# A gated graph network on one core: last two pairs side by side, h kept in place, adj in quarters, its square by seven products

## The chip, the cores and the metric

The kernel runs on one core of one Trainium2 chip. Its engines are TensorE (PE: matmuls; PEld: loading their weights), VectorE (DVE), ScalarE (ACT), GpSimd (POOL) and SyncE (SP, which issues the DMAs here). The metric is device time in microseconds (us), the median of several runs. One more execution was taken with the hardware profiler; all views come from that one.

## The reference, cut to what matters

```python
# x: (32, 512, 128), adj: (512, 512), all fp32
def prop(x): return einsum('ij,bjc->bic', adj, x)
y = [x, A x, A^2 x, A^3 x, A x, A^2 x, A^3 x]          # both adjacency inputs are adj
x = layernorm(x + sum_k y[k] @ W0[k])                   # layer 0
h = x
for _ in range(5):                                      # layer 1
    m  = einsum('nm,bmd->bnd', adj, h)                  # m_in = m_out = m
    u3 = h @ u3_w.T + u3_b
    z  = sigmoid([m, m] @ w3_w.T + w3_b + u3)
    r  = sigmoid([m, m] @ w4_w.T + w4_b + u3)
    hv = tanh([m, m] @ w5_w.T + w5_b + (r * h @ u5_w.T + u5_b))
    h  = (1 - z) * h + z * hv
out = layernorm(x + h)
```

## The kernel before

Two batches make a pair `q` (16 pairs). A tile of one batch is 128 x 512 fp32: nodes on the partitions (four chunks of 128 side by side) or, "turned", channels on the partitions and the 512 nodes along the row.

**Planner.** Nothing is issued directly. Each piece of work is an `Op` with an engine, an assumed length, the operations that it follows, slots that it takes and gives back (`take`, `give`), and a key. `Plan.run` (line 69) goes through time and gives each free engine the ready operation with the lowest key whose slots are free; what it emits in that order is the program's order on every engine. The keys are `32 * q` for a pair, plus 30 and 20 a step inside. Slots are the tiles in `slots` (line 151): eight PSUM banks, `hT` (turned h), `X` (h with nodes on the partitions), `S` (sums for products), `m` (adj times h), `uT`, `rh`, `z`, `rest`, `d` (DRAM), `two` (products under way at a time: 2), `inside` (pairs in layer 1 at a time: 5).

**Products.** `seven` (line 374) multiplies 2 x 2 blocks with seven products instead of eight: each product is two or four matmuls, p1, p3, p5 and p6 add up in one bank, and between them ACT copies its state out (`Q`, c1, c3, c5); DVE adds these copies to the other banks (d2, d5, d7). p3 must wait for c1, p5 for c3, p7 for d5. Its sums (`S`) come from POOL. It is used for adj times x (`adj_product`), for layer 0's weights (line 530) and for adj squared times U (line 586). For the latter adj squared is made once, by 16 matmuls of 128x512 (line 272) from four transposes of adj.

**A step** (`pair`, line 693; `gates`, line 654). u3s times h (line 707), adj times h by `seven`, then for each batch: w4s times m, DVE adds uT (line 664), ACT's sigmoid, DVE times h gives rh; w3s times m, DVE adds uT (line 671), ACT's sigmoid z (line 673) and a second sigmoid of the negated input, `rest` (line 675), that POOL multiplies by h (line 678); w5s times m and u5s times rh into one bank, Tanh (line 685), DVE times z (line 687) and plus rest (line 689) into a new `hT`. For the next step's products h must have its nodes on the partitions: for all pairs but the last by a DVE block transpose and two DMA passes through DRAM (`turn`, line 343), for pair 15 (`TURNED = 15`) by four PE transposes and an ACT copy (lines 739 to 742). After the fifth step POOL adds h0 into a tile `y` (line 752), `norm` (line 309) takes moments on DVE for each of four chunks (lines 318, 319), the power on POOL, and the final scale and shift on ACT (line 328); SP stores.

**Start.** SP loads x of pair 0 (two DMAs), adj in four chunks of 128 rows (line 200), then the weights. DVE makes the sums `T` of adj and the layer 0 weights.

Of the kernel before, what the change touches and what calls it, by code (L numbers as in the profile page):

```python
# [11 lines left out]
ALU = mybir.AluOpType  # L12
PSUM = bass.MemoryType.PSUM

P = 128
# [7 lines left out]
TURNED = 15  # L23
# [17 lines left out]
class Plan:  # L41
# [5 lines left out]
    LATE = {"PE": 0.2, "DVE": 0.1, "ACT": 0.1, "POOL": 0.1, "SP": 0.0, "-": 0.0}  # L47

# [5 lines left out]
    def __call__(self, engine, us, emit, after=(), take=(), give=(), key=0.0, late=None):  # L54
        late = self.LATE[engine] if late is None else late
        op = Op(engine, us, emit, [a for a in after if a is not None], take, give, key, late)
        self.ops.append(op)
        return op
# [62 lines left out]
def gnn_resnorm_kernel(  # L121
# [26 lines left out]
    def tiles(tag, n, shape=(P, N), pool=work):  # L148
# [5 lines left out]
        xg=tiles("xg", 1, (P, 2, NK, P)),  # L154
        xT=tiles("xT", 4),
        tT=tiles("tT", 4),
        U=tiles("U", 2, (P, NK, 2, P)),
        Y=tiles("Y", 2, (P, 2, NK, P)),
        h0=tiles("h0", 5, (P, 2, NK, P)),
        hT=tiles("hT", 10),  # L160
        X=tiles("X", 2, (P, 2, P * NK)),
        m=tiles("m", 7),
        uT=tiles("uT", 4),
        rh=tiles("rh", 3),
        z=tiles("z", 2),
        rest=tiles("rest", 4),
        S=tiles("S", 2, (P, 7, H, P)),
        Q=tiles("Q", 2, (P, 3, HN)),
        v=tiles("v", 5),
        y=tiles("y", 4, (P, NK, P)),  # L170
        two=[None] * 2,
        inside=[None] * 5,
# [18 lines left out]
    def load_x(q):  # L191
        for b in range(2):
            nc.sync.dma_start(plan[f"xg{q}"][:, b], x[2 * q + b].rearrange("(p k) c -> p k c", k=NK))

    def loaded_x(q, key):
        return plan("SP", 0.84, lambda: load_x(q), take=[("xg", f"xg{q}")], key=key, late=3.0)

    x_in = {0: loaded_x(0, -99.0)}
    at_in = [
        plan("SP", 0.46, lambda k=k: nc.sync.dma_start(at[:, k], adjT[:, k]), key=-90.0 + k, late=4.5)  # L200
        for k in (0, 2, 1, 3)
    ]
# [12 lines left out]
    w_of = lambda: plan["w0"].rearrange("p b f -> p (b f)")[:, : 7 * P]  # L215
    w0_in = plan("SP", 0.45, lambda: nc.sync.dma_start(w_of(), w0), take=[("X", "w0")], key=-70.0, late=6.5)

# [10 lines left out]
    w0_ready = plan("DVE", 2.3, layer0_weights, after=[w0_in], give=[("X", "w0")], key=-40.0)  # L228
# [4 lines left out]
    def gate_weight(src, name):  # L233
        halves = lambda: plan[name][:, : 2 * P].rearrange("p (h o) -> p h o", h=2)
        w = const.tile([P, P], F32, tag=name, name=name)
        emit = lambda: nc.sync.dma_start(halves(), src.rearrange("(h c) o -> c h o", c=P))
        got = plan("SP", 0.45, emit, take=[("rh", name)], key=-60.0, late=6.5)
        emit = lambda: nc.vector.tensor_tensor(w, halves()[:, 0, :], halves()[:, 1, :], ALU.add)
        ready.append(plan("DVE", 0.28, emit, after=[got], give=[("rh", name)], key=-30.0))
        return w  # L240
# [18 lines left out]


    an_ready = []
    for km in range(NK):
        emit = lambda km=km: transposes(plan[f"ba{km}"], lambda k: at[:, k, chunk(km)])
        tr = plan("PE", 0.44, emit, after=at_in, take=[("bank", f"ba{km}"), ("m", f"an{km}")], key=20.0)
        emit = lambda km=km: nc.scalar.copy(plan[f"an{km}"], plan[f"ba{km}"])
        an_ready.append(plan("ACT", 0.59, emit, after=[tr], give=[("bank", f"ba{km}")], key=20.0))
    squares, squared = [], []
    for k in range(NK):
        for km in range(NK):

            def emit(k=k, km=km):
                nc.tensor.matmul(  # L272
                    plan[f"bs{k}"],
                    lhsT=plan[f"an{km}"][:, chunk(k)],
                    rhs=at[:, km, :],
                    start=(km == 0),
                    stop=(km == NK - 1),
                )

            squares.append(  # L280
                plan(
                    "PE",
                    0.86,
                    emit,
                    after=an_ready + squares[-1:],
                    take=[("bank", f"bs{k}")] if km == 0 else [],
                    give=[("m", f"an{j}") for j in range(NK)] if k == km == NK - 1 else [],
                    key=21.0,
                )
            )  # L290
        emit = lambda k=k: nc.vector.tensor_copy(at2[:, k, :], plan[f"bs{k}"])
        squared.append(plan("DVE", 0.69, emit, after=squares[-1:], give=[("bank", f"bs{k}")], key=21.0))


    A11, A12 = at2[:, :H, :HN], at2[:, H:, :HN]
    A21, A22 = at2[:, :H, HN:], at2[:, H:, HN:]
    A2_sums = []
    for i, (a, b, op) in enumerate(
        (
            (A21, A22, ALU.add),  # L300
            (at2S[:, 0], A11, ALU.subtract),
            (A11, A21, ALU.subtract),
            (A12, at2S[:, 1], ALU.subtract),
        )
    ):
        emit = lambda i=i, a=a, b=b, op=op: nc.vector.tensor_tensor(at2S[:, i], a, b, op)  # L306
        A2_sums.append(plan("DVE", 0.69, emit, after=squared + A2_sums[-2:], key=21.0))

    def norm(n, name, src_of, dst_of, after, give, key):
# [22 lines left out]
        for i in range(n):  # L332
            got.append(plan("DVE", 0.45, lambda i=i: moments(i), after=after, key=key))
        p = plan("POOL", 1.75, power, after=got, key=key)
        over = []
        for i in range(n):
            last = i == n - 1
            over.append(
                plan("ACT", 0.45, lambda i=i: apply(i), after=[p] + over, give=give if last else [], key=key)
# [3 lines left out]
    def turn(src_of, dst_of, name, after, key, take=()):  # L343
# [15 lines left out]
        t = plan("DVE", 0.7, blocks, after=after, take=[("v", f"v{name}")], key=key)  # L359
# [14 lines left out]
    def seven(name, after, us, terms, product, keep, end, key, take=(), give=()):  # L374
# [4 lines left out]
        Qn = f"Q{name}"  # L379
        banks = {i: f"p{i}{name}" for i in "abc"}  # L380
        half = lambda i: plan[banks[i]][:, :HN]

        def pe(i, bank, first, last, after, take=()):
            left, right, ready = terms[i]
            emit = lambda: product(half(bank), left(), right(), first, last)
            return plan("PE", us, emit, after=list(after) + list(ready), take=take, key=key)

        def out(what, bank, after, *i, give=()):
            engine, us, emit = what(*i)
            return plan(engine, us, lambda: emit(half(bank)), after=after, give=give, key=key)  # L390

        Q_of = lambda i: lambda: plan[Qn][:, i]
        kept = lambda i, bank, after: out(keep, bank, after, i, Q_of(i))
        take = [("two", f"two{name}"), ("Q", Qn), ("bank", banks["a"]), ("bank", banks["c"])] + list(take)
        p1 = pe(0, "a", True, False, after, take=take)
        c1 = kept(0, "a", [p1])
        p2 = pe(1, "b", True, True, [p1], take=[("bank", banks["b"])])
        d2 = out(end, "b", [p2, c1], 0, 0, Q_of(0), give=[("bank", banks["b"])])
        p3 = pe(2, "a", False, False, [c1])
        c3 = kept(1, "a", [p3])  # L400
        p4 = pe(3, "c", True, False, [p1])
        p5 = pe(4, "a", False, False, [c3])
        c5 = kept(2, "a", [p5])
        d5 = out(end, "c", [p4, c5], 1, 1, Q_of(2))
        p6 = pe(5, "a", False, True, [c5])
        c6 = out(end, "a", [p6], 1, 0, None, give=[("bank", banks["a"])])
        p7 = pe(6, "c", False, True, [d5])
        d7 = out(end, "c", [p7, c3, d5, d2], 0, 1, Q_of(1), give=[("bank", banks["c"]), ("Q", Qn), ("two", f"two{name}")])
# [414 lines left out]
```

## Time and profile before

| | |
|---|---|
| median of 3 runs | 1528.29 us (1528.23 to 1528.51) |
| the profiled execution, its own time | 1527.84 us |
| its span, first to last instruction | 1526.0 us |
| busy: PE, DVE, ACT, POOL | 1500.0, 958.8, 830.6, 773.2 us |
| mean granted TensorE clock | 0.996 |
| DMA share | 31.6% of 16 engines |

An engine's busy time is the time in which it works on some instruction; "idle before" is the time just before an instruction, with what ended it. The timeline merges equal neighbours (x4 is four records; an fp32 matmul leaves two, a transpose one). In the table by stretches each row has the stretch, its length, the busy time and number of instructions of each engine, TensorE's granted clock, the DMA share and GB/s. The gates' part of the groups:

```profile
L678 POOL TENSOR_TENSOR rest<-rest,hT 128x512 f32<-128x512 f32 x160 | 202.6, 1270 | 346.0 <-ACT rest L675 330.7
...
L413 ACT COPY Q<-bank 128x256 f32<-128x256 f32 x384 | 143.2, 373 | 293.5 <-PE bank L456 255.8
...
L687 DVE TENSOR_TENSOR bank<-bank,z 128x512 f32<-128x512 f32 x160 | 111.4, 697 | 122.3 <-ACT bank L685 121.2
...
L685 ACT ACTIVATE bank<-bank,hv_b 128x512 f32<-128x512 f32 x160 | 106.0, 663 | 80.4 <-PE bank L659 80.3
...
L673 ACT ACTIVATE z<-bank 128x512 f32<-128x512 f32 x160 | 94.5, 598 | 64.6 <-DVE bank L671 64.4
```

POOL's product of 1270 ns mostly waits for ACT's second sigmoid (330.7 of 346.0 us); all of these run while PE does other pairs' matmuls.

### The profile page before, as it was taken

To read this page: it belongs to the slowest core of one execution; us is meant where nothing else is said; L and a number is where in the kernel's file an instruction comes from. 1 tells how busy PE (TensorE), PEld (TensorE's weight loads), DVE (VectorE), ACT (ScalarE), POOL (GpSimd) and SP (SyncE) were. 2 spreads that over 40 slices of the span, in tenths; PEclk is the share of its full clock that TensorE was granted. 3 is DMA by queue.
4 is the path that set the end of the run, shared out by engine and by line. 5 is a ranking of instruction groups with operands and counts; after the bars stand their busy time and mean duration, and the time that the engine had idled before them with its cause. 6 is when DMAs were issued, how large, how long until landed. Compare 5 with 4: busy or idle time off the path is not lost.

```text
span 1526.0 us, 20599 instructions
## 1 busy us (share of the span) xinstructions
PE 1500.0 (98%) x6200; PEld 1031.2 (68%) x6200; DVE 958.8 (63%) x2039; ACT 830.6 (54%) x1768; POOL 773.2 (51%) x1090
## 2 busy tenths in 40 slices
PE   8999999999999999999999999999999999999995
PEld 6877666666766677676666766677676666766552
DVE  3556576667566665657667566665657666665754
ACT  2364545656465654645656465654546655555644
POOL 3454554545554465554545654464554545634534
PEclk9999999999999999999999999999999999999998
DMA  2122423325144342423414144242423413231220
GB/s 88 50 55 70 111 60 90 106 71 131 44 107 113 76 120 55 125 68 90 132 47 133 43 110 112 72 122 56 130 64 90 132 45 92 59 107 45 61 51 27
DMA packets 160190, 128.19 MB, mean 84 GB/s; under 512 B 18384, under 2 KB 124880, under 8 KB 160080
## 3 DMA queue, kind: packets, MB, share of 16 engines
q1 hardware_dynamic: 160080, 126.89, 31.6%
q8 instruction: 49, 0.80, 0.2%
q14 instruction: 61, 0.50, 0.1%
HBM read 64.42 MB, written 62.39 MB: 83 GB/s over the span
## 4 chain that ended last, share of the span: by engine, by line
PE 96%; issue 1%; DVE 1%; DMA 1%; POOL 1%; ACT 0%; SPq 0%; ACTq 0%; POOLq 0%
PE bank L456 38%; PE bank L659 35%; PE bank L707 9%; PE bank L530 6%; PE bank L586 6%; PE bank L272 1%; PE bank L258 1%; DMA at<-in_adjT 0%; SPq L350 0%; POOL rest L678 0%; DMA v<-d 0%; POOL y L752 0%; DVE st L318 0%; DVE at2S L306 0%; DVE mv L319 0%
## 5 line engine op out<-in xcount | busy, mean ns | idle before, releaser
L678 POOL TENSOR_TENSOR rest<-rest,hT 128x512 f32<-128x512 f32 x160 | 202.6, 1270 | 346.0 <-ACT rest L675 330.7
L456 PE MATMUL bank<-T,S 128*128 128x256 f32 x1392 | 345.1, 380 | 1.5 <-ACT Q L413 1.5
L456 PEld LDWEIGHTS bank<-T,S 128*128 128x128 f32 x1392 | 261.7, 190 | 88.1 <-ACT Q L413 30.3
L413 ACT COPY Q<-bank 128x256 f32<-128x256 f32 x384 | 143.2, 373 | 293.5 <-PE bank L456 255.8
L456 PE MATMUL bank<-at,S 128*128 128x256 f32 x864 | 221.8, 379 | 0.0
L456 PEld LDWEIGHTS bank<-at,S 128*128 128x128 f32 x864 | 160.8, 190 | 45.0 <-issue 25.1
L421 DVE TENSOR_TENSOR m<-bank,Q 128x256 f32<-128x256 f32 x240 | 100.3, 418 | 140.6 <-PE bank L456 94.9
L687 DVE TENSOR_TENSOR bank<-bank,z 128x512 f32<-128x512 f32 x160 | 111.4, 697 | 122.3 <-ACT bank L685 121.2
L664 DVE SCALAR_TENSOR_TENSOR bank<-bank,b4s,uT 128x512 f32<-128x512 f32 x160 | 120.3, 753 | 91.1 <-PE bank L659 86.4
L707 PE MATMUL bank<-hT,u3s 128*128 128x512 f32 x320 | 160.9, 596 | 0.0
L659 PE MATMUL bank<-m,w4s 128*128 128x512 f32 x320 | 157.9, 592 | 0.0
L659 PE MATMUL bank<-m,w5s 128*128 128x512 f32 x320 | 155.0, 592 | 0.0
L659 PE MATMUL bank<-m,w3s 128*128 128x512 f32 x320 | 154.0, 592 | 0.0
L659 PE MATMUL bank<-rh,u5s 128*128 128x512 f32 x320 | 153.2, 592 | 0.0
L685 ACT ACTIVATE bank<-bank,hv_b 128x512 f32<-128x512 f32 x160 | 106.0, 663 | 80.4 <-PE bank L659 80.3
L666 ACT ACTIVATE bank<-bank 128x512 f32<-128x512 f32 x160 | 92.3, 581 | 84.7 <-DVE bank L664 83.9
L712 ACT ACTIVATE uT<-bank,ub3s 128x512 f32<-128x512 f32 x160 | 109.8, 688 | 51.2 <-PE bank L707 48.9
L448 POOL TENSOR_TENSOR S<-X 128x256 f32<-128x256 f32 x128 | 91.7, 727 | 77.7 <-PE bank L456 32.5
L673 ACT ACTIVATE z<-bank 128x512 f32<-128x512 f32 x160 | 94.5, 598 | 64.6 <-DVE bank L671 64.4
L671 DVE SCALAR_TENSOR_TENSOR bank<-bank,b3s,uT 128x512 f32<-128x512 f32 x160 | 118.8, 750 | 11.3 <-PE bank L659 10.8
L667 DVE TENSOR_TENSOR rh<-bank,hT 128x512 f32<-128x512 f32 x160 | 107.7, 681 | 14.5 <-ACT bank L666 13.3
L689 DVE TENSOR_TENSOR hT<-bank,rest 128x512 f32<-128x512 f32 x160 | 107.5, 681 | 7.4 <-POOL rest L678 1.7
(113 smaller groups left out, 2250.6 us busy)
## 6 DMA issues: line engine op xcount, KB each, us to landing
d<-v SPq DMA_DIRECT2D x824, 64.0 KB, 1.8
X<-d SPq DMA_DIRECT2D x150, 256.0 KB, 2.7
v<-d SPq DMA_DIRECT2D x56, 256.0 KB, 2.7
xg<-in_x SPq DMA_DIRECT2D x32, 256.0 KB, 2.7
out<-y SPq DMA_DIRECT2D x32, 256.0 KB, 2.2
at<-in_adjT SPq DMA_DIRECT2D x4, 256.0 KB, 5.3
X<-in_w SPq DMA_DIRECT2D x1, 448.0 KB, 6.4
rh<-in_w SPq DMA_DIRECT2D x3, 128.0 KB, 6.3
```

Source lines behind the costliest of these rows:

```text
L413: return "ACT", 0.37, lambda src: nc.scalar.copy(Q(), src)
L456: nc.tensor.matmul(dst, lhsT=left[:, k, :], rhs=right[:, k, :], start=(first and k == 0), stop=(last and k == H - 1), skip_group_check=True,)
L659: mm = lambda dst, w, src, first, last: nc.tensor.matmul(plan[dst], lhsT=w, rhs=plan[src], start=first, stop=last)
L664: emit = lambda: nc.vector.scalar_tensor_tensor(plan[pr], plan[pr], b4s, plan[uT], ALU.add, ALU.add)
L667: emit = lambda: nc.vector.tensor_tensor(plan[rh], plan[pr], plan[h], ALU.mult)
L671: emit = lambda: nc.vector.scalar_tensor_tensor(plan[pz], plan[pz], b3s, plan[uT], ALU.add, ALU.add)
L678: emit = lambda: nc.gpsimd.tensor_tensor(plan[rest], plan[rest], plan[h], ALU.mult)
L685: emit = lambda: nc.scalar.activation(plan[ph], plan[ph], AF.Tanh, bias=hv_b)
L687: emit = lambda: nc.vector.tensor_tensor(plan[ph], plan[ph], plan[z], ALU.mult)
L689: emit = lambda: nc.vector.tensor_tensor(plan[h_new], plan[ph], plan[rest], ALU.add)
L707: emit = lambda bn=bn, hb=h[b]: nc.tensor.matmul(plan[bn], lhsT=u3s, rhs=plan[hb], start=True, stop=True)
L712: emit = lambda bn=bn, uT=uT: nc.scalar.activation(plan[uT], plan[bn], AF.Identity, bias=ub3s)
```

## The change

It has several parts.

- **Keys.** A pair's key is taken from a list, `KEYS`; a step adds `LONG` = 20. The last two keys are 464 and 478, so pairs 14 and 15 are nearly in step; the others are 22 to 38 apart. `two` goes from 2 to 3, `inside` from 5 to 7. The planner takes an engine to be free a little before an operation is done (`OVERLAP`).
- **Turning h.** `ON_PE = {14: 1, 15: 3}`: PE transposes for pair 14's last step and pair 15's last three; all else by DVE and DMA. After the last step of these two pairs nothing is copied: DVE adds h0 from the PSUM bank.
- **Start.** adj is loaded in quarters (256 rows by 256 columns), in the order x's first half, two quarters, x's second half, two quarters; the first product waits only for its quarter.
- **Square of adj** by `seven`: seven products of four 128x256 matmuls, with four DVE sums of the transposed adj.
- **In place.** `seven` copies its first sum to the result's own tile and adds there (`into`); `Q` is gone. `gates` computes `h + z * (hv - h)` in h's own tile: Tanh, DVE minus h, DVE times z, then plus h on POOL, or on DVE for the last `QUICK` = 2 pairs. `rest`, the second sigmoid and POOL's product are gone, as are the tiles `y`: the result is put in h0's tile. X is held for each batch by itself.

```diff
-TURNED = 15
+ON_PE = {14: 1, 15: 3}
+QUICK = 2
+KEYS = [20.0, 58.0, 80.0, 112.0, 148.0, 180.0, 208.0, 240.0, 272.0, 304.0, 334.0, 366.0, 396.0, 426.0, 464.0, 478.0]
+LONG = 20.0
...
+    OVERLAP = {"DVE": 0.08, "ACT": 0.1, "POOL": 0.04}
...
+        overlap = min(self.OVERLAP.get(engine, 0.0), us / 2)
+        us, late = us - overlap, late + overlap
...
-        xg=tiles("xg", 1, (P, 2, NK, P)),
+        xg=tiles("xg", 2, (P, 2, NK, P)),
...
-        tT=tiles("tT", 4),
+        tT=tiles("tT", 5),
...
-        Y=tiles("Y", 2, (P, 2, NK, P)),
-        h0=tiles("h0", 5, (P, 2, NK, P)),
-        hT=tiles("hT", 10),
-        X=tiles("X", 2, (P, 2, P * NK)),
-        m=tiles("m", 7),
-        uT=tiles("uT", 4),
+        Y=tiles("Y", 4, (P, 2, NK, P)),
+        h0=tiles("h0", 4, (P, 2, NK, P)),
+        hT=tiles("hT", 8),
+        X=tiles("X", 4),
+        uT=tiles("uT", 6),
...
-        z=tiles("z", 2),
-        rest=tiles("rest", 4),
+        z=tiles("z", 4),
+        m=tiles("m", 5),
...
-        two=[None] * 2,
-        inside=[None] * 5,
+        two=[None] * 3,
+        inside=[None] * 7,
...
-        plan("SP", 0.46, lambda k=k: nc.sync.dma_start(at[:, k], adjT[:, k]), key=-90.0 + k, late=4.5)
+    def load_adj(i, j, key):
+        k, c = slice(i * H, (i + 1) * H), slice(j * HN, (j + 1) * HN)
+        emit = lambda: nc.sync.dma_start(at[:, k, c], adjT[:, k, c])
...
+        a = plan("SP", 0.42, emit, take=[("xg", "xg0")], key=-99.0, late=2.9)
+        b = plan("SP", 0.42, lambda: load_x(0, 1), key=-91.0, late=4.0)
...
+    in11, in21 = load_adj(0, 0, -95.0), load_adj(1, 0, -94.0)
+    at_in = [in11, in21, load_adj(0, 1, -90.0), load_adj(1, 1, -90.0)]
...
+    def into(dst, cols, plus=None):
+        def first(i, j):
+            if plus is None:
+                return "ACT", COPY[cols], lambda src: nc.scalar.copy(dst(i, j), src)
+            return "DVE", ADD[cols], lambda src: nc.vector.tensor_tensor(dst(i, j), src, plus(i, j), ALU.add)
+        def second(i, j):
+            return "DVE", ADD[cols], lambda src: nc.vector.tensor_tensor(dst(i, j), src, dst(i, j), ALU.add)
...
+    def square_product(dst, left, right, first, last):
+        for j in range(H):
+            for k in range(H):
                 nc.tensor.matmul(
-                    plan[f"bs{k}"],
-                    lhsT=plan[f"an{km}"][:, chunk(k)],
-                    rhs=at[:, km, :],
...
+                    dst[:, j, :],
+                    lhsT=left[:, k, chunk(j)],
+                    rhs=right[:, k, :],
...
+    _, squared = seven("sq", an_ready, 1.72, terms, square_product, into(dst, N), 21.0, whole, give=give)
...
-        emit = lambda: nc.scalar.activation(plan[rest], plan[pz], AF.Sigmoid, scale=-1.0)
-        t = plan("ACT", 0.59, emit, after=[t, zs], give=[("bank", pz)], key=key + 0.5)
-        emit = lambda: nc.gpsimd.tensor_tensor(plan[rest], plan[rest], plan[h], ALU.mult)
-        keep = plan("POOL", 1.27, emit, after=[t], key=key + 0.5)
...
-        emit = lambda: nc.vector.tensor_tensor(plan[ph], plan[ph], plan[z], ALU.mult)
-        t = plan("DVE", 0.69, emit, after=[t, zs], give=[("z", z)], key=key + 0.8)
-        emit = lambda: nc.vector.tensor_tensor(plan[h_new], plan[ph], plan[rest], ALU.add)
...
+        emit = lambda: nc.vector.tensor_tensor(plan[ph], plan[ph], plan[h], ALU.subtract)
+        t = plan("DVE", 0.69, emit, after=[t], key=key + 0.8)
+        emit = lambda: nc.vector.tensor_tensor(plan[z], plan[ph], plan[z], ALU.mult)
+        t = plan("DVE", 0.69, emit, after=[t, zs], give=[("bank", ph)], key=key + 0.8)
+        engine, us = (nc.vector, 0.69) if quick else (nc.gpsimd, 1.27)
+        emit = lambda: engine.tensor_tensor(plan[h], plan[z], plan[h], ALU.add)
+        return plan("DVE" if quick else "POOL", us, emit, after=[t], give=[("z", z)], key=key + 0.8)
...
+            by_dma = s < STEPS - ON_PE.get(q, 0)
...
+                y = lambda b=b: h0_of(b)
+                if by_dma:
+                    emit = lambda b=b, X_new=X_new, y=y: nc.gpsimd.tensor_tensor(
+                        fit(y(), True), X_new(b), fit(y(), True), ALU.add
+                    )
+                    t = plan("POOL", 1.27, emit, after=[t], give=[("X", Xb)], key=key + 17)
+                else:
+                    emit = lambda y=y, bn=bn: nc.vector.tensor_tensor(
+                        y(), plan[bn].rearrange("p (k c) -> p k c", k=NK), y(), ALU.add
+                    )
+                    t = plan("DVE", 0.69, emit, after=[t], give=[("bank", bn)], key=key + 17)
```

## The prediction, made before the changed kernel was run

> **What bounds the kernel now.** I read three views in this order: the page's sums and chain, the busy time by stretches, then the waits and the timeline at the two ends. First the page:
>
> ```profile
> span 1526.0 us, 20599 instructions
> ...
> PE 1500.0 (98%) x6200; PEld 1031.2 (68%) x6200; DVE 958.8 (63%) x2039; ACT 830.6 (54%) x1768; POOL 773.2 (51%) x1090
> ...
> PE 96%; issue 1%; DVE 1%; DMA 1%; POOL 1%; ACT 0%; SPq 0%; ACTq 0%; POOLq 0%
> ```
>
> TensorE is busy 98% of the span and carries 96% of the chain of waits, so outside the ends a saving must take matmuls away. The stretches (length, then busy time of PE, PEld, DVE, ACT, POOL) show where its 26.0 us of idle time lie:
>
> ```profile
> 0.00:10.00 10.00, 5.29 (x18) 4.31 (x19) 2.10 (x4) 3.21 (x5) 4.19 (x11) 1.00 0.75 238
> 10.00:40.00 30.00, 29.98 (x145) 21.57 (x144) 9.68 (x27) 7.78 (x19) 10.46 (x15) 1.00 0.12 33
> 40.00:60.00 20.00, 18.48 (x129) 16.11 (x128) 12.33 (x33) 4.66 (x12) 9.24 (x14) 1.00 0.27 67
> 60.00:100.00 40.00, 39.95 (x201) 30.30 (x200) 19.93 (x52) 24.66 (x51) 22.61 (x36) 1.00 0.24 61
> 100.00:1400.00 1300.00, 1299.46 (x5367) 895.38 (x5366) 843.34 (x1774) 722.40 (x1547) 674.43 (x947) 1.00 0.34 89
> ...
> 1480.00:1500.00 20.00, 15.75 (x50) 9.22 (x49) 10.45 (x29) 10.83 (x22) 11.14 (x16) 0.91 0.24 69
> 1500.00:1510.00 10.00, 9.08 (x29) 5.08 (x28) 4.88 (x8) 3.46 (x8) 0.19 (x1) 1.00 0.00 0
> 1510.00:1526.00 16.00, 2.97 (x12) 1.22 (x10) 5.68 (x20) 6.70 (x14) 8.20 (x12) 0.71 0.09 33
> ```
>
> From 100 to 1400 us PE is idle 0.54 us: nothing to win there, much to lose. The first 10 us hold 4.7, 40 to 60 hold 1.5, the end holds the rest. What PE waits for after 1440:
>
> ```profile
> PE bank L258 <- DVE hT L689: 6.4, 3, 4.2
> PE bank L456 <- ACT Q L413: 1.8, 4, 0.5
> ```
>
> These are the last pair alone: its transposes wait for its own h, its products for their own copies. The timeline of both ends (start, length, in brackets the wait ahead):
>
> ```profile
> 6.65 2.07 PE L456 MATMUL bank<-at,xg 128*128 128x256 f32 x4 [1.13 <-DMA at<-in_adjT]
> ...
> 1492.73 1.05 PE L258 MATMUL bank<-ident,hT 128*128 128x128 f32 x4 [4.25 <-DVE hT L689]
> ...
> 1501.20 1.13 PE L456 MATMUL bank<-T,S 128*128 128x256 f32 x4 [0.46 <-ACT Q L413]
> ...
> 1502.79 1.13 PE L456 MATMUL bank<-T,X 128*128 128x256 f32 x4 [0.46 <-ACT Q L413]
> ...
> 1510.83 0.66 ACT L685 ACTIVATE bank<-bank,hv_b 128x512 f32<-128x512 f32 x1 [0.33 <-PE bank L659]
> ...
> 1514.48 0.66 PE L258 MATMUL bank<-ident,hT 128*128 128x128 f32 x4 [0.74 <-DVE hT L689]
> ...
> 1521.27 1.65 ACT L328 ACTIVATE y<-y,shift,rstd 128x128 f32<-128x128 f32 x4 [0.26 <-POOL shift L325]
> ```
>
> **What the Trainium skill says.** "TensorE: Matmul & The Clock Gate", section "Wait — 56ns, not 53.3ns?", gives a matmul's spacing as columns by clock plus about 2.5 ns. The trace agrees: 68 records of 256 columns run in 14.68 us on the chain at 991.19, 216 ns each where 213 is the pure array time, two records to a matmul. The section "What's actually happening" has the array at half clock until it has been busy about 3.4 us: at 6.65 four records take 2.07 us, at 1003.11 four take 1.03. That is paid in time, so an earlier start pays it earlier, not less. "PSUM — Partial Sum Buffer", section "Engine vs sequencer instructions", says that ScalarE, VectorE and GpSimd work strictly in order; in the trace DVE's 16 moment instructions of the two batches from 1515.73 to 1519.00 run one behind another. "DMA: Bandwidth & Descriptors", section "Specifications", puts line rate at 512 B and more; adj in quarters has rows of 1 KB instead of 2, so I charge nothing, and no run here shows 1 KB rows.
>
> **The change, part by part**, against the profiled execution's 1527.84 us, of which 1526.0 are the span.
>
> *Square of adj.* A 128x512 matmul takes 0.86 us (from 1504.62 to 1506.34 go two), a 128x256 one 0.43. Out go 16 of the first, 13.8; in come 28 of the second, 12.1: -1.7. The four sums on DVE (0.69 each) and four copies of a whole bank on ACT (about 0.59) lie beside other matmuls: in the new order the products of pair 0 and the w products stand between those of the square.
>
> *Transposes of h on PE.* Before: the last pair's 10 x 4. Now pair 14's last step and pair 15's last three: 8 x 4. Eight fewer at 0.11 (8 go from 13.00 to 13.88): -0.9. What the two new DMA turns cost lies beside the other pair's matmuls. All other matmuls are the same by count.
>
> *Start.* PE's first wait (3.59) is for the first half of x and stays. Then the first product waits 1.13 for a load of adj that stands third in SP's queue; its quarter now stands second, and the transposes of x's second half follow it. The gain is between 0 (if what held the first adj load holds the quarter) and 1.1 (all of it). T's second sum needs the last quarter, at the end of the same 1.5 MB, so that comes no earlier; before it, PE now has 4.3 us of matmul work instead of 3. I take -0.6. The 1.5 us at 40 to 60 are w products with nothing between them; such rows stand in the new order too. I take 0, from -1.5 to +1.5.
>
> *Last two pairs.* In the new order pair 14's matmuls stand between pair 15's nearly to the end; after pair 14's last transposes PE has 12 us left. Before pair 15's earlier turned steps, 4.3 us of matmuls stand between the u5s product and the transposes of the same h. The way back is Tanh 0.66, three DVE operations of 0.69 and some 0.4 of handing over, 3.1: covered by 1.2. The products of the last `seven` have u3s products and pair 14's transposes between them. So all waits after 1440 but the last two go: 8.2 - 1.42 - 0.74 = 6.0 of idle time in seven waits, and each costs more from start to start (1502.79 - 1501.20 is 1.59 for 0.86 of work, 0.73 where 0.46 is idle): 7.4 with 0.2 for each. Late next is DVE: pair 14's two sums and 16 moment instructions, 1.4 + 3.3 us, stand in its queue ahead of pair 15's last gate additions, with two additions of m between; the first u5s would be late by 0.3, the second by 0.7. I take 1.0 back: -6.4, from -8 to -3.
>
> *Behind the last gate.* Before, from the Tanh at 1510.83 to 1526.0: 15.2. Now DVE has six gate operations instead of four, in the order sub, sub, mult, mult, add, add, from 1511.5 at about 0.7: 1515.7. Transposes to 1516.5; the sum from PSUM replaces ACT's copy (0.59) and POOL's sum (1.27), 0.7: 1517.2. Eight pairs of moments at 0.41: 1520.5 (before 1519.0, as DVE was free at 1514.4 and only waited for POOL). POOL 0.4 later for 1.8: 1522.7. ACT then has five of the final operations behind it in its order, not four, at 0.39: 1524.8; and 3.1 for the store, as from 1522.9 to 1526.0: 1527.9. +1.9, from +1.2 to +2.5.
>
> *Gates, all pairs.* ACT loses 160 second sigmoids (94 us of its 831) and POOL's product moves to the end of the chain: for 14 pairs Tanh, sub, mult, then POOL's 1.27 before h can be used, against Tanh, mult, add. Nothing of this is on PE's path unless the order leaves too little between. It leaves, for the inner pairs, 1.4 us at one place and otherwise 3.1 or more beyond that chain before u3s, and 4.5 before the next products (before: 1.9 and 3.7). Where a matmul needs an eviction, only one step of 0.86 stands between at about 400 places, against about 250 before; those 250 cost 0.54 in all. In-place sums change no count: `seven`'s last copy and its DVE additions stay one for one. DVE gets 20 sums for the last two pairs (14 us). I take +0.7 for the middle, from -0.5 to +15.
>
> Sum: -1.7 - 0.9 - 0.6 + 0 - 6.4 + 1.9 + 0.7 = -7.0, so 1520.8 profiled. The profiled execution is 0.45 under the median of the runs, 1528.29; so 1521.3.
>
> **Rivals.** *All gaps close* (0.2): start -1.1, 40 to 60 -1.5, tail -7.4, behind it +1.4, no loss inside: -11.2, 1517. For it: every wait removed has work of the other pair in its place. Against: DVE's queue at the end. *The tail gives it back* (0.15): pair 14's norms and pair 15's gates collide on DVE in both last steps; of 7.4 only 3.4 stay, and the end costs 2.4: -1.7 - 0.9 - 0.6 - 3.4 + 2.4 + 0.7 = -3.5, 1525. For it: before, one such collision made a wait of 4.25 where the bare chain (Tanh, two DVE operations) is 2.4. *DVE and POOL delay the middle* (0.13): h now passes through DVE, DVE and POOL. Of the stretches with 10 us of matmul work, DVE's instructions fill over 0.9 in eight, at most 0.99, before in none (at most 0.89). At 0.2 us for each of the 70 steps of 14 pairs it loses 14 instead of 0.7: +6.3, 1534.6. From 0.15 a step it is slower than before by 0.2%. Against: ACT is freer, POOL's fullest stretch falls from 1.42 to 1.14, and the same kind of order ran 1300 us without a gap.
>
> **How the numbers follow.** Forecast 0.52, with its own range 1517 to 1525. A median of this kernel can tell 0.2%, 3.1 us, from no change: below 1525.2 is faster. The forecast is there nearly always, the second for certain, the third half the time: 0.77. Same: 0.10. Slower: 0.13. The range goes from 1515 to 1531, which leaves under one in ten on each side.
>
> **What would show it.** The stretches after: PE idle under 1.5 between 100 and 1400; no wait of a transpose above 1 us but the last two; PE's wait for adj below 1.1; from the last Tanh to the end about 17. Transposes waiting for h over 2 us before the end speak for the third case, waits for DVE or for POOL's hT spread over the middle for the last. I am wrong if the middle's idle time exceeds 5 us.

## The result and the profile after

| | before | after |
|---|---|---|
| median of 20 runs each | 1528.24 us (1526.98 to 1529.96) | 1525.51 us (1522.49 to 1529.07) |
| ratio after to before, 95% interval | | 0.9984 (0.9977 to 0.9991) |
| the profiled execution, and its span | 1527.84, 1526.0 us | 1526.63, 1524.5 us |

The change wins 2.7 us, where 7 were forecast. First the page of the kernel after: span, busy times, chain of waits.

```profile
span 1524.5 us, 20210 instructions
...
PE 1498.4 (98%) x6216; PEld 1034.4 (68%) x6216; DVE 975.6 (64%) x2068; ACT 753.5 (49%) x1610; POOL 750.6 (49%) x1068
...
PE 90%; DVE 4%; DMA 2%; SPq 2%; ACT 1%; POOL 1%; issue 1%; ACTq 0%; POOLq 0%; DVEq 0%
```

PE is still busy 98% of the span, but its share of the chain fell from 96% to 90%: DVE, DMA and SP's queue now stand on it. Where, the busy time by stretches of the kernel after shows (stretch, length, PE, PEld, DVE, ACT, POOL, clock, DMA share, GB/s):

```profile
0.00:10.00 10.00, 5.25 (x16) 3.93 (x17) 1.30 (x2) 2.83 (x4) 2.95 (x9) 1.00 0.79 244
...
40.00:60.00 20.00, 19.10 (x139) 17.84 (x138) 10.16 (x33) 7.84 (x21) 11.39 (x21) 1.00 0.26 67
...
100.00:1400.00 1300.00, 1295.33 (x5300) 886.79 (x5299) 841.71 (x1775) 652.94 (x1399) 663.39 (x932) 1.00 0.33 88
...
1480.00:1500.00 20.00, 20.00 (x79) 13.36 (x78) 15.66 (x33) 9.76 (x19) 3.23 (x5) 1.00 0.00 0
```

Between 1480 and 1500 PE has no gap left, where it had 4.25 us. Between 100 and 1400 it is idle 4.67 us, where it was 0.54. Idle time is less than what is lost, so the table below counts from the start of each PE record to the start of the next and takes off the time that its columns need at full clock (213 ns for a record of 256 fp32 columns, as the prediction has it). It is worked out from the records of the two profiles; the wait of 3.6 us ahead of the first record, which both have, is left out, and "last gate" is the start of the last u5s record.

| us | before | after | difference | forecast |
|---|---|---|---|---|
| matmuls and transposes at full clock | 1470.3 | 1467.7 | -2.6 | -1.7 - 0.9 |
| lost, 0 to 100 | 10.3 | 9.8 | -0.5 | -0.6 + 0 |
| lost, 100 to 1400 | 18.2 | 25.1 | +7.0 | +0.7 |
| lost, 1400 to 1450 | 0.4 | 0.7 | +0.3 | |
| lost, 1450 to the last gate | 9.6 | 1.0 | -8.5 | -6.4 |
| behind the last gate's start | 15.0 | 17.8 | +2.9 | +1.9 |

The rows give -1.4, the spans -1.5. (Some 17 us of the middle's loss are the 3 ns by which every record exceeds its columns, in both kernels.) One row is out of line: the middle. PE's waits between 100 and 1400 in the kernel after (line waited for, us, times, longest):

```profile
PE bank L487 <- ACT S L467: 1.4, 2, 1.0
PE bank L487 <- DVE m L352: 1.1, 2, 0.6
PE bank L487 <- DVE tT L352: 0.7, 2, 0.6
PE bank L700 <- DVE rh L708: 0.7, 1, 0.7
PE bank L624 <- DVE v L349: 0.6, 1, 0.6
PE bank L487 <- ACT m L348: 0.2, 1, 0.2
```

Nine waits on several lines: no engine is too slow everywhere; some order fails at a few places. One of them on the timeline of the kernel after:

```profile
901.44 1.27 POOL L792 TENSOR_TENSOR h<-X,h 128x512 f32<-128x512 f32 x1 [5.50 <-DMA X<-d]
902.67 2.49 POOL L729 TENSOR_TENSOR hT<-z,hT 128x512 f32<-128x512 f32 x2
905.12 1.27 POOL L792 TENSOR_TENSOR h<-X,h 128x512 f32<-128x512 f32 x1
...
906.42 0.29 DVE L283 BATCH_NORM_STATS2 st<-h 128x6 f32<-128x128 f32 x1 [0.52 <-POOL h L792]
...
907.24 0.39 DVE L352 TENSOR_TENSOR tT<-bank,tT 128x256 f32<-128x256 f32 x1
...
907.69 0.70 PE L487 MATMUL bank<-at,S 128*128 128x256 f32 x2 [0.58 <-DVE tT L352]
```

After a pair's last step POOL adds h0 for each of the two batches. It stands idle for 5.50 us until the first batch's turned h lands in X, does that sum, two additions of other gates, and ends the second sum at 906.39. The moments of the final norm (L283) stand at the head of DVE's queue and hold it for 0.52 us; behind them stands the addition that `seven` needs before its next product, and PE waits 0.58 us. That VectorE, ScalarE and GpSimd work strictly in order is in the Trainium skill, "PSUM — Partial Sum Buffer", section "Engine vs sequencer instructions", and this trace agrees. The same wait of DVE between 100 and 1440 us in three kernels: before, after, and f1_last_late of the experiments:

```profile
DVE st L318 <- POOL y L752: 1.0, 3, 0.4
```

```profile
DVE st L283 <- POOL h L792: 13.0, 10, 3.1
```

```profile
DVE st L283 <- POOL h L792: 0.2, 1, 0.2
```

POOL's last sums wait for the landing of the last step's turn, so the question was whether the turn lands later than the planner assumed.

### The profile page after: what moved, and what is told of

Read it like the earlier page. It is cut to its first block, busy times and chain, and to the rows that moved or that the text cites. A ratio compares the mean times of both kernels' runs of the same rounds, so it can differ in the third digit from the quotient of the medians.

```text
span 1524.5 us, 20210 instructions
## 1 busy us (share of the span) xinstructions
PE 1498.4 (98%) x6216; PEld 1034.4 (68%) x6216; DVE 975.6 (64%) x2068; ACT 753.5 (49%) x1610; POOL 750.6 (49%) x1068
## 4 chain that ended last, share of the span: by engine, by line
PE 90%; DVE 4%; DMA 2%; SPq 2%; ACT 1%; POOL 1%; issue 1%; ACTq 0%; POOLq 0%; DVEq 0%
PE bank L487 35%; PE bank L700 32%; PE bank L746 8%; PE bank L624 6%; PE bank L565 6%; DMA X<-d 1%; SPq L315 1%; PE bank L423 1%; PE bank L272 1%; DVE bank L724 1%; DVE st L283 0%; DVE z L726 0%; POOL h L792 0%; DVE mv L284 0%; ACT h L293 0%
## 5 line engine op out<-in xcount | busy, mean ns | idle before, releaser
L729 POOL TENSOR_TENSOR hT<-z,hT 128x512 f32<-128x512 f32 x140 | 177.4, 1270 | 279.0 <-DVE z L726 274.8
L487 PE MATMUL bank<-at,S 128*128 128x256 f32 x880 | 226.8, 381 | 3.8 <-ACT S L467 1.4
L348 ACT COPY m<-bank 128x256 f32<-128x256 f32 x320 | 118.4, 370 | 216.4 <-PE bank L487 215.3
L487 PEld LDWEIGHTS bank<-at,S 128*128 128x128 f32 x880 | 165.3, 190 | 76.6 <-issue 39.7
L352 DVE TENSOR_TENSOR m<-bank,m 128x256 f32<-128x256 f32 x240 | 100.0, 417 | 171.8 <-PE bank L487 106.5
L724 DVE TENSOR_TENSOR bank<-bank,hT 128x512 f32<-128x512 f32 x160 | 110.0, 692 | 117.7 <-ACT bank L721 116.7
L700 PE MATMUL bank<-m,w3s 128*128 128x512 f32 x320 | 158.4, 593 | 0.0
L700 PE MATMUL bank<-rh,u5s 128*128 128x512 f32 x320 | 157.1, 594 | 0.7 <-DVE rh L708 0.7
L323 DVE STREAM_TRANSPOSE v<-hT 128x512 f32<-128x512 f32 x152 | 105.3, 698 | 10.2 <-POOL hT L729 9.1
L726 DVE TENSOR_TENSOR z<-bank,z 128x512 f32<-128x512 f32 x160 | 108.3, 682 | 2.2
```

What stands on the lines that cost most here:

```text
L348: return "ACT", COPY[cols], lambda src: nc.scalar.copy(dst(i, j), src)
L487: nc.tensor.matmul(dst, lhsT=left[:, k, :], rhs=right[:, k, :], start=(first and k == 0), stop=(last and k == H - 1), skip_group_check=True,)
L700: mm = lambda dst, w, src, first, last: nc.tensor.matmul(plan[dst], lhsT=w, rhs=plan[src], start=first, stop=last)
L724: emit = lambda: nc.vector.tensor_tensor(plan[ph], plan[ph], plan[h], ALU.subtract)
L726: emit = lambda: nc.vector.tensor_tensor(plan[z], plan[ph], plan[z], ALU.mult)
L729: emit = lambda: engine.tensor_tensor(plan[h], plan[z], plan[h], ALU.add)
```

## The experiments

Five rounds each; the kernel before ran beside them (medians 1528.77, 1528.78, 1528.70 and 1529.07 us in the four sets). "Idle" is PE's from 100 to 1400 us. Three explanations of the middle stood at the start: late landing of the last step's turn (A), POOL's place in the gates' chain (B), the uneven keys (C).

**y1_tail_only.** The kernel before with one part of the change: the last pair's key and where the last two pairs turn h.

```diff
-TURNED = 15
+ON_PE = {14: 1, 15: 3}
+LAST = 462.0
-        key0 = 32.0 * q
+        key0 = 32.0 * q if q < NP - 1 else LAST
+            by_dma = s < STEPS - ON_PE.get(q, 0)
...
+                    emit = lambda b=b, y=y, bn=bn: nc.vector.tensor_tensor(
+                        plan[y], plan[bn].rearrange("p (k c) -> p k c", k=NK), plan[f"h0{q}"][:, b], ALU.add
+                    )
```

> The kernel before with the part at the end alone: pair 15's key 14 after pair 14's instead of 32, PE transposes for the last step of pair 14 and the last three of pair 15, the last sum from PSUM on DVE; gates, sums, start, square and the other keys as before. Theory A (the part at the end brings its whole gain, about 6 us, and what was lost in the middle belongs to other parts): middle idle time of PE (100 to 1400) stays under 1.5 us, time 1521.5 to 1523.5, faster than the changed kernel's 1525.5. Rival (the gain at the end is itself what crowds the kernel): 1525 to 1528.

Measured: 1520.39 us, ratio 0.9946 (0.9933 to 0.9958); idle 0.54, as before. Lost from 1450 to the last gate: 1.4 instead of 9.6. So the last two pairs bring their gain alone, three times the whole change's; the rest of the change gives some 5 us back.

**e2_old_gates.** The changed kernel with the gates of before (second sigmoid, POOL's product beside the path, two DVE operations behind the Tanh).

```diff
+        emit = lambda: nc.scalar.activation(plan[rest], plan[pz], AF.Sigmoid, scale=-1.0)
+        emit = lambda: nc.gpsimd.tensor_tensor(plan[rest], plan[rest], plan[h], ALU.mult)
-        emit = lambda: nc.vector.tensor_tensor(plan[ph], plan[ph], plan[h], ALU.subtract)
-        emit = lambda: nc.vector.tensor_tensor(plan[z], plan[ph], plan[z], ALU.mult)
-        emit = lambda: engine.tensor_tensor(plan[h], plan[z], plan[h], ALU.add)
+        emit = lambda: nc.vector.tensor_tensor(plan[ph], plan[ph], plan[z], ALU.mult)
+        emit = lambda: nc.vector.tensor_tensor(plan[h], plan[ph], plan[rest], ALU.add)
```

> The changed kernel with the gates of before (second sigmoid, POOL's product beside the chain, DVE's product and sum), h still written in place. Theory B (POOL's sum at the end of the gate chain makes turned h late and so costs the middle its 7 us): middle idle time falls from 4.7 to under 2, time 1519 to 1522. Theory A (late work in DVE's and ACT's queues, whatever the gates): middle idle time stays at 3 to 6 and the 160 more sigmoids cost nothing or little, time 1525 to 1531.

Measured: 1532.55 us, ratio 1.0022 (1.0015 to 1.003); idle 6.7, both above even the range that A gave. Undoing the gates makes the middle worse (30.6 us lost there, 25.1 in the change), so B falls.

**e3_even_keys.** The changed kernel with the first 15 keys spaced evenly.

```diff
-KEYS = [20.0, 58.0, 80.0, 112.0, 148.0, 180.0, 208.0, 240.0, 272.0, 304.0, 334.0, 366.0, 396.0, 426.0, 464.0, 478.0]
+KEYS = [20.0, 51.7, 83.4, 115.1, 146.9, 178.6, 210.3, 242.0, 273.7, 305.4, 337.1, 368.9, 400.6, 432.3, 464.0, 478.0]
```

> The changed kernel with its first 15 keys evenly 31.7 apart (20 to 464), the last 478 as it was. Theory C (the uneven keys put too much in some stretches): middle idle time under 2, time 1519 to 1523. Theory A: idle time stays at 3 to 7, time 1525 to 1531.

Measured: 1526.57 us, ratio 0.9987 (0.998 to 0.9994); idle 5.7, in A's range. C falls.

**f1_last_late.** The changed kernel; the planner takes the last step's turn to land 5.0 us after its issue instead of 2.8. Same operations, another order.

```diff
-    def turn(src_of, dst_of, name, after, key, take=(), give=()):
+    def turn(src_of, dst_of, name, after, key, take=(), give=(), late=2.8):
...
-                    t = turn(h_of, lambda Xb=Xb: plan[Xb], nm, [d] + read[b], key + 15, [("X", Xb)], give)
+                    t = turn(h_of, lambda Xb=Xb: plan[Xb], nm, [d] + read[b], key + 15, [("X", Xb)], give, 5.0 if last else 2.8)
```

> The changed kernel with one number changed: the planner takes a last step's turned h to land 5.0 us after its issue, not 2.8, so that POOL's last sum and the 16 moments of a pair's norm stand later in the queues of POOL and DVE. Theory A (POOL's last sum waits for a DMA that lands later than planned, the moments behind it hold DVE, and an addition that PE needs stands behind them): the waits of products for DVE behind moments go (4 of the 10 places in the middle, 2 to 3 us), time 1522 to 1524. Rivals B and C: no change, 1525 to 1526.

Measured: 1518.83 us, ratio 0.9932 (0.9918 to 0.9945). The middle in its stretches:

```profile
100.00:1400.00 1300.00, 1298.91 (x5320) 889.25 (x5318) 840.30 (x1776) 657.06 (x1406) 664.90 (x938) 1.00 0.33 89
```

Idle 1.09 where the change has 4.67; of the 7.0 us lost in the middle 5.5 are back (19.6 against 25.1). The time is below A's own 1522 to 1524. One assumed time in the order takes away most of what was lost. Since it draws the whole order anew, the rival that any new order would do (D) is taken up next.

**f2_other_late, f3_both_late.** The other steps' turns at 3.4 us: alone, and together with f1's 5.0.

```diff
-                    t = turn(h_of, lambda Xb=Xb: plan[Xb], nm, [d] + read[b], key + 15, [("X", Xb)], give)
+                    t = turn(h_of, lambda Xb=Xb: plan[Xb], nm, [d] + read[b], key + 15, [("X", Xb)], give, 2.8 if last else 3.4)
```

```diff
-                    t = turn(h_of, lambda Xb=Xb: plan[Xb], nm, [d] + read[b], key + 15, [("X", Xb)], give)
+                    t = turn(h_of, lambda Xb=Xb: plan[Xb], nm, [d] + read[b], key + 15, [("X", Xb)], give, 5.0 if last else 3.4)
```

> The changed kernel with one number of the planner altered: a turn of any step but the last is taken to land 3.4 us after its issue, not 2.8; the last step's stays at 2.8. The operations are the same, only their order moves. Theory A (the last step's fetch lands later than the order assumes, POOL's last sum is late, the final moments hold DVE's and ACT's queues): the fault is untouched, so 1523 to 1527 us and 4 to 6 us of idle time of PE between 100 and 1400. Rival D (any turn that lands late costs, the last step's is nothing special; what f1_last_late won is that the order was drawn anew): 1518 to 1521 us and under 2.5 us of idle time.

> The changed kernel with both numbers altered: 5.0 us for the last step's turn, 3.4 for the others. Theory A: the last step's number does nearly all of it, so within 1.5 us of f1_last_late's 1518.8, 1517.3 to 1520. Rival D: another 2 us or more below, under 1516.8.

Measured: f2 1521.54 us, ratio 0.9958 (0.9944 to 0.9971), idle 3.2; f3 1516.29 us, ratio 0.992 (0.9906 to 0.9934), idle 0.5. f2 falls between the two theories: DVE's moments still wait for POOL's last sums (12.4 us in 12 waits), yet 4 us are won. f3 is in D's range and below A's. But of the 4.9 us between the profiles of f2 and of the change, 2.4 stand in the first 100 us, which this number hardly touches, and so do 2.3 of the 3.5 us between those of f1 and f3. In the middle f2 lost 23.5 us where the change lost 25.1, and f3 18.6 where f1 lost 19.6. So the other steps' number is worth 1.0 to 1.6 us there and the last step's about 5. A new order by itself isn't what helps: five orders with 2.8 us for the last step (the change, e2, e3 and f2, and e1 below) lost 23.5 to 30.8 us in the middle, the two with 5.0 (f1, f3) lost 19.6 and 18.6. A holds in the main and is too narrow.

**h1_no_moments.** The changed kernel in its own order, with the moments of batches 0 to 27 replaced by a write that waits for nothing (the final norm of these batches is not computed).

```diff
+            if name[:2] == "1_" and int(name[2:]) < 28:
+                nc.vector.memset(mv[:, i, :], 1.0)
+                return
```

> The changed kernel, same planned order, but the two moment instructions of the final norm of batches 0 to 27 are left out; in their place a small write of ones to their result, which waits for no data. So these 28 batches' final mean and variance are not computed. POOL's last sums and the final applications still run, and the fetch lands as before. Theory A with the moments as the holder: DVE no longer stands still for POOL's last sum, so PE's idle time between 100 and 1400 falls from 4.7 to about 2.5 us (ACT's copies of the last sums still wait for late fetches) and the time to 1519 to 1523 us. If the moments hold nobody: 4 to 6 us of idle time and 1524 to 1527 us.

Measured: 1522.49 us, ratio 0.9956 (0.9943 to 0.9968); idle 3.4. The time is in A's range, the idle time is not. In the same order the middle loses 23.1 us without the moments and 25.1 and 24.5 with them (the change, and after_again below), so the way over DVE's moments is worth 1.4 to 2 us of the 7. What remains is mostly PE waiting 2.0 us for ACT's copies S, and ACT waits 13.3 us there for fetches. Those copies read the X of an earlier step, so this is a second way, for other turns than the last step's. A third is POOL's own queue, where sums and gate additions stand behind the late last sum, as at 902.67 above; no run takes it away alone. Nor does the wait of the moments measure the loss: e3 has 4.6 us of it and is idle 5.7, m1 below has 9.7 and is idle 2.2.

**m1_last_mid.** As f1, with 3.6 us: 0.8 us of room instead of 2.2.

```diff
-                    t = turn(h_of, lambda Xb=Xb: plan[Xb], nm, [d] + read[b], key + 15, [("X", Xb)], give, 5.0 if last else 2.8)
+                    t = turn(h_of, lambda Xb=Xb: plan[Xb], nm, [d] + read[b], key + 15, [("X", Xb)], give, 3.6 if last else 2.8)
```

> As f1_last_late, with 3.6 us for the last step's turn where that has 5.0 and the changed kernel 2.8: 0.8 us of room. If the turn comes late by what the whole of it takes above the order's 6.7 us (0.6 in the median, 2.4 in one of ten), the middle gets a part back: PE idle 1.5 to 3.5 us between 100 and 1400, DVE's moments still waiting 3 to 9 us for POOL's last sums (13 in the changed kernel, 0.2 in f1_last_late), 1519.5 to 1523 us. If the landing of the fetch alone were it (0.1 us later in the median), 0.8 us would be room enough: idle under 1.5 us, 1518 to 1519.5.

Measured: 1520.33 us, ratio 0.994 (0.9927 to 0.9952), idle 2.2; DVE's moments wait 9.7 us. A part comes back (20.9 us lost in the middle). How late are the turns? With the records matched in the order in which the planner emits them, a last step's turn takes 6.5 us in the median before and 8.6 after, from the end of DVE's block transposition to the landing in X (one of ten above 7.5 and 10.8); in f1_last_late it takes 8.5. The turns are no faster there, they only have room. The fetch alone moved little (2.73 to 2.87); the rest stands ahead of it, where the DMAs of neighbouring turns queue on SP: the first store waits 0.9 us in the median, where it waited 0.03. The order's bare 1.76 + 1.8 + 0.35 + 2.8 = 6.7 us leaves out such waits, but the planner adds those that it foresees. So the fair measure is each turn against the planner's own time for it: over 0.5 us later were 2 of 30 last turns before, 16 of 28 after, 7 in m1_last_mid and none in f1_last_late. Of the other steps' turns it was 41 of 120 before and 41 of 124 after, so these were late already in a kernel that had no idle time in the middle.

**e1_no_overlap.** The changed kernel without the planner's new credit for overlapping operations.

```diff
-    OVERLAP = {"DVE": 0.08, "ACT": 0.1, "POOL": 0.04}
+    OVERLAP = {}
```

> The changed kernel without the planner's new credit (0.04 to 0.1 us for each operation of DVE, ACT and POOL that overlaps the next on its engine). If that credit packed the order so that late turns stand in PE's way: PE idle under 2 us between 100 and 1400, near 1520 us. If the room was lost through the other parts (buffers by batch, seven pairs in flight, sums in place): PE idle 4 us or more, 1524 us or more.

Measured: 1529.64 us, ratio 1.0 (0.9992 to 1.0008), idle 7.2. The credit is not what took the room away; without it the kernel is slower.

**g1_old_last_gate.** For the end: f1_last_late with the gates of before in the last pair's last step only (the lines of e2).

> f1_last_late with the gates of the kernel before (a second sigmoid on ACT, its product with h on POOL beside the path, two DVE operations behind the Tanh) in the last step of the last pair alone. If the six DVE operations between the last Tanh and the transposes are what made the way behind the last gate longer than before, two of 0.7 us go: 1.4 us less from the last Tanh to the end, about 1517.4 us where f1_last_late has 1518.8. If the end is held by something else (the moments, POOL's powers, ACT's five applications): no difference, 1518.3 to 1519.3.

Measured: 1517.57 us, ratio 0.9929 (0.9917 to 0.9942). The time is the expected one, the reason only half of it: from the Tanh to the end it takes 15.7 us instead of 17.1, but the two more sigmoids stand in ACT's queue ahead of the Tanh, which starts 2.35 us behind the start of its u5s product instead of 1.39. From the start of the last gate's last product that nets 0.4 us, and 0.7 us more is lost ahead of it. The profiles lie 2.8 us apart because g1 lost 3.3 us less in the first 100 us, so that the time is the expected one is luck.

**g3_kept_part.** f1_last_late; in the last pair's last step DVE makes (z - 1) h while it waits for the Tanh, and two operations follow instead of three.

```diff
+            emit = lambda: nc.vector.scalar_tensor_tensor(plan[rest], plan[z], 1.0, plan[h], ALU.subtract, ALU.mult)
+            emit = lambda: nc.vector.tensor_tensor(plan[ph], plan[ph], plan[z], ALU.mult)
+            emit = lambda: nc.vector.tensor_tensor(plan[h], plan[ph], plan[rest], ALU.subtract)
```

> f1_last_late with another form of the last gate in the last step of the last pair: DVE works out (z - 1) h while it waits for the Tanh, so two DVE operations, not three, stand behind the Tanh, and ACT's queue stays as it is (in g1_old_last_gate two more sigmoids stood in front of the Tanh, which came 0.96 us later behind the u5s product; from the Tanh to the end it took 1.3 us less). If the DVE operations behind the Tanh are what made the end longer: 1.4 us less than f1_again, from the Tanh to the end 15.7 us, not 17.1. If the end moves with something else: the same as f1_again within 0.5 us.

The measure beside it was f1_again, the same kernel as f1_last_late:

> f1_last_late once more, as the measure for the two below. If the start differs by chip: near 1516.8; if not, 1518.8. PE idle under 1.5 us between 100 and 1400 either way.

Measured: g3 1516.67 us, ratio 0.9922 (0.991 to 0.9934); f1_again 1518.44, ratio 0.9934 (0.9922 to 0.9946). The end of g3 on the timeline:

```profile
1497.82 0.69 DVE L720 SCALAR_TENSOR_TENSOR rest<-z,hT 128x512 f32<-128x512 f32 x1 [0.18 <-ACT z L715]
1498.07 1.21 ACT L726 ACTIVATE bank<-bank,hv_b 128x512 f32<-128x512 f32 x2
...
1498.74 1.30 DVE L730 TENSOR_TENSOR bank<-bank,z 128x512 f32<-128x512 f32 x2 [0.23 <-ACT bank L726]
1499.94 1.28 DVE L732 TENSOR_TENSOR hT<-bank,rest 128x512 f32<-128x512 f32 x2
```

h is ready 3.15 us behind the Tanh's start; in f1_again it was 4.37 us. From the Tanh to the end: 15.2 against 16.4 us, 1.2 less where 1.4 were expected. The medians differ by 1.8 us, but their intervals overlap; it is the profile that carries this verdict.

**k1_best.** f3_both_late with g3's last gate.

> The two together: f3_both_late (5.0 us for the last step's turn, 3.4 for the others) with the last gate of g3_kept_part. If both effects are real and stand in different places, they add: 1.4 us under f3_both_late's 1516.3, about 1514.9, PE idle under 1.5 us between 100 and 1400, 15.7 us from the last Tanh to the end. If not, 1516 to 1517.

Measured: 1516.97 us, ratio 0.9922 (0.9911 to 0.9934), idle 0.85, from the Tanh to the end 15.7 us. The shorter end is there, but the time isn't under f3's, in another set: what was expected if the effects do not add. In the profiles k1 lost 1.9 us more than f3 in the first 100 us. f3, g3 and k1 cannot be ranked by these runs; each is about 0.8% faster than before and beats the change too.

**after_again.** The changed kernel once more.

> The changed kernel once more, beside the three below. Its profiles so far had half-clock products up to 10 us into the span, and those of the last four kernels had none behind 8; if that is a matter of the chip and not of the kernel, the loss of the first 100 us is here 7 to 8 us too, and the time 2 us lower, near 1523.5; if not, 1525.5. Between 100 and 1400 PE should again be idle 4 to 6 us, since the same fetches land late.

Measured: 1525.06 us, ratio 0.998 (0.9974 to 0.9987), idle 3.9, a little under the expected range; DVE's moments wait 13.7 us for POOL. The loss of the first 100 us was 10.4 us here and 8.0 for f1_again on the same chip, so it isn't the chip alone that sets it. The same transposes of adj, first here and then in f1_again:

```profile
9.86 3.53 PE L272 MATMUL bank<-ident,at 128*128 128x128 f32 x16
```

```profile
9.04 1.91 PE L272 MATMUL bank<-ident,at 128*128 128x128 f32 x16
```

The trace's clock records begin with the full clock (the views show 1.00 ahead of it too), at 13.2 us here and at 8.6 in f1_again. PE's last wait ahead of that ends at 7.3 and 6.9 us, so it was busy for 5.9 and 1.7 us until the full clock came, and not for one time like the 3.4 us of the prediction. Of the fourteen profiles of the changed family, the six in which it begins before 9 us lost 6.9 to 8.0 us in the first 100, the eight in which it begins after 9 us 8.6 to 10.4. Most of that spread is when the full clock came, and why it came when it did is open.

## Why the prediction was right or wrong

- **The step that failed: the term +0.7 for the middle ("Gates, all pairs", -0.5 to +15).** It measured +7.0 in the table above. The working weighed the gates' chain and counted the steps between a product and its eviction. It gave no price to the landing of the turns, though the trace of before had it, and though it had said of the last pairs that moments in DVE's queue delay additions behind them. The runs put this in its place: the last step's turns take 8.6 us in the median where they took 6.5, and 16 of 28 land over 0.5 us behind the order's own time; POOL's last sum comes late, it and DVE's moments hold their queues, and PE waits for what stands behind. With room for these turns f1_last_late has 5.5 of the 7.0 us back and ends at 1518.8, 2.5 us below the forecast. Of the ways from a late sum to PE only that over the moments was taken away alone (h1_no_moments, 1.4 to 2 us); how the rest divides, and why f1 also ends PE's waits for ACT's copies (0.2 us instead of 1.4), is not shown. The criterion of the text, an idle time of over 5 us, was nearly met (4.7 and 3.9); as a bound it was too loose, since 1.7 us of time went with each us of idle time (7.0 for 4.13 more).
- **Square and transposes, -2.6:** right to the tenth (1470.3 to 1467.7).
- **Last two pairs, -6.4:** -8.5, beyond its range. The mechanism was right, y1_tail_only shows it alone (-8.2), and the size too small: the 1.0 us put back for DVE's queue did not come, and the working left out the half clock. In the trace of before the granted clock is 0.50 from 1492.85 to 1496.27, straight behind the wait of 4.25 us (four transposes take 1.05 us at 1492.73 and 0.66 at 1514.48, both among the prediction's lines). That cost 1.8 us. In the kernel after no such wait is left ahead of the last gate, and the clock is full from 11.3 to 1509.7.
- **Behind the last gate, +1.9:** +2.5 counted from the Tanh (15.2 to 17.7). The moments end 9.7 us behind it, POOL 11.9, ACT's five operations 14.0, all as worked out, but in part by luck: h was ready at 4.4 and not at 4.9, and the eight transposes of it ran at half clock, 1.97 us, where the sum has 0.8. The store took 3.7 us instead of 3.1. g3_kept_part shows that the third DVE operation is worth 1.2 of it. The clock makes the end differ between runs of one kernel, too: from the Tanh to the end f1_last_late took 17.1 us with its transposes at half clock (1.97), f1_again 16.4 at full clock (1.26).
- **Start, -0.6:** -0.5 in the one pair of profiles, but not as told. These are PE's first records of the kernel after:

```profile
3.61 1.09 PE L272 MATMUL bank<-ident,xg 128*128 128x128 f32 x4 [3.61 <-DMA xg<-in_x]
4.49 2.08 PE L487 MATMUL bank<-at,xg 128*128 128x256 f32 x4
7.71 1.12 PE L272 MATMUL bank<-ident,xg 128*128 128x128 f32 x4 [1.14 <-DMA xg<-in_x]
```

  The first product starts at 4.49 instead of 6.65 and waits for nothing, but x's second half, now behind two quarters of adj, lands at 7.66 instead of 4.07, and PE waits 1.14 for that: the wait changed its name. (The 1 KB rows, for which nothing was charged, cost nothing that shows: the quarters landed 5.0 us behind their issue in the median, the chunks of before 5.3.) Over the profiles of the changed family the first 100 us lose 6.9 to 10.4 us, so a gain of 0.5 isn't told apart from none.
- **The rival "DVE and POOL delay the middle"** had the right place and the wrong mechanism: with the old gates the middle loses more (30.6 us in e2_old_gates), not less.

Open: which part of the change left the order without room. Gates, keys and overlap credit, each undone alone, are out; buffers by batch, seven pairs in flight and sums in place weren't tried one by one. With room for the last turns the middle still loses 1.4 us more than before (19.6 against 18.2), with room for all of them 0.4 (18.6).

## What to carry to other kernels

Where a static order puts an operation that waits for a DMA into an in-order queue, its assumed landing is a price: take the whole way (every issue on the DMA queue, each pass, the landing) from the trace, at its slow end and not at its median, and give the room to the waits that hold a queue which others need. Room for one kind of transfer was worth 6.7 us here (1525.5 to 1518.8), over twice what the whole change brought, and it costs nothing but order. And ask of each saving, before the next is added to it, whether it stands when made alone: y1_tail_only was faster than the whole.

## What the hardware showed that was not expected

DVE's addition hT<-z,hT, which has both inputs in SBUF, took 0.68 us, but 1.26 and 1.11 us at two places in the kernel after. DVE and POOL there:

```profile
1379.61 1.26 DVE L729 TENSOR_TENSOR hT<-z,hT 128x512 f32<-128x512 f32 x1
...
1382.05 1.11 DVE L729 TENSOR_TENSOR hT<-z,hT 128x512 f32<-128x512 f32 x1
```

```profile
1379.59 0.73 POOL L474 TENSOR_TENSOR S<-X,X 128x256 f32<-128x256 f32 x1
...
1381.89 0.72 POOL L474 TENSOR_TENSOR S<-X,S 128x256 f32<-128x256 f32 x1
```

POOL started 0.02 and 0.16 us earlier, and DVE ended 0.55 us behind POOL's end both times, as if it had worked only when POOL was done. The Trainium skill says this, "SBUF — State Buffer", section "SBUF: two separate sides": the two engines share a pair of ports, and of a DVE operation with two SBUF inputs and a POOL operation that reads SBUF, the one that starts first has it for its whole length. The trace agrees. In six profiles of the changed family (the kernel after, e3, f1, f2, f3 and h1), 85 such additions beside an idle POOL took 0.69 us at most, and every one of the 14 that took over 0.8 us stood beside a POOL operation; the two DVE operations of the gates that read PSUM took 0.68 and 0.69 us beside POOL in the median, 0.68 and 0.70 without it. The gates of before had no operation of this kind. In the kernel after, both additions stand in DVE's queue ahead of an rh that it makes at 1383.75, and the u5s product that needs this rh waits 0.7 us for it: one of the nine waits of the middle.
